# Graph-attention stack on one core: the projections at the ends of whole blocks, computed as seven products of quarters in place of eight

## The chip, the cores and the metric

The kernel runs on one core of a Trainium2 chip. The metric is the device time of one launch in microseconds, the median of several runs. TensorE (PE) multiplies matrices, VectorE (DVE) and ScalarE (ACT) do element-wise work, GpSimd (POOL) does a few small tasks here, and SyncE's queue (SP) issues nearly all DMAs.

## What is computed

A node matrix x (3327 x 256, f32) goes through four graph layers over one adjacency matrix. Each layer adds its result to x and normalises the rows. The last of the four holds three attention passes, so the kernel counts six layers: "0" (cosine attention), "1" (GAT), "2" (query/key attention), and "3a", "3b", "3c" (GAT). The part that matters is a GAT pass:

```python
def _gat_layer(h, adj, W, a):
    Wh = h @ W
    f1 = Wh @ a[:F_out]
    f2 = Wh @ a[F_out:]
    e = jax.nn.leaky_relu(f1 + f2.T, ALPHA)
    att = jnp.where(adj > 0, e, NEG_INF)
    att = jax.nn.softmax(att, axis=1)
    h_prime = att @ Wh
    return jax.nn.elu(h_prime)
```

The kernel uses att @ (h @ W) = (att @ h) @ W: it multiplies the unprojected h with the attention weights first, and projects the finished rows with the 256 x 256 matrix W afterwards. This projection is what the change is about.

## The kernel before

**Tiling.** The rows are padded to 3328 = 26 tiles of 128 (`NT`). Output rows are made in seven blocks (`NB`): b = 0 to 5 of 512 rows (4 tiles), b = 6 of 256 rows (2 tiles). A block runs over the 26 source tiles j in 26 steps. The main loop (`for s, (L, b, j)` over `steps`, L1276) is the same for all six layers.

**One step of a GAT layer.** ScalarE makes `re` (L657) and VectorE makes the weights `e` of tile j, 128 x 512 (L668). TensorE multiplies: four matmuls of 257 columns, one for each row tile of the block, into the PSUM tiles `po` (L1337); the 257th column sums the weights. Steps are prepared `LA` = 2 steps ahead and more where buffers allow: `e` has five buffers, `re` three. Layers "2" and most of "0" use products of quarters already (Strassen, in Winograd's form): there `products` (L751, matmuls at L779) does two source tiles at once with 14 matmuls of 128 or 129 columns.

**The end of a block.** When the 26th step is issued, `finish(L, b, pos)` (L871) is appended to `pending`, and `advance()` runs it up to its next `yield` once per step. So the end of block b is spread over the steps of block b + 1. For a GAT layer the pieces are: reciprocals of the sums (L959, L962) and scaled copies `p4` (L963); `turn` (L827): two ScalarE copies into `planes` (L834), a transposing DMA (L837), a few steps of waiting, two VectorE copies into `pT4` (L844); then, one row tile a step, `projected(k)` (L986), and after it `activated(k)` (L1020). `projected` for one tile is

```python
pm = bank("pproj")
for h in range(2):
    nc.tensor.matmul(pm[:, :D], pT[:, h, :], w[L.w][:, h, :], start=(h == 0), stop=(h == 1))
src = pm[:, :D]
```

with ELU read out of PSUM: ScalarE's relu and exp (L1007, L1008) and VectorE's maximum (L1011 in hidden layers, L1014 with the residual in "1" and "3c"). Hidden layers then compute the scores for the next layer (`scores`, L591) and a running sum (L862). Layers "1" and "3c" take row statistics (L883, L884) and normalise (L1050). Layer "1" also turns the normalised rows, projects them for layer "2" (`pv`, L1080, L1087) and stores sums for layer "2" (`combine`, L690, L713).

At j = 22 (L1373; at j = 25 in the last block of layer "1") what is left in `pending` is run to its end.

**Pools and order.** `ps_b` has three PSUM banks, shared by `pproj`, `pv`, `psr` and others. The tag `x4k` has two buffers of 4 KB a partition, shared by `planes`, `pT4`, `tsum` and others; `acc` has two. After a hand-ordered start the instructions of each engine are put in order by a scheduler at build time, which keeps dependencies and tile lifetimes; the order of the text is only its input. Each engine then runs its list strictly in order.

Of the kernel before, what the change touches and what calls it, by code (L numbers as in the profile page):

```python
# [8 lines left out]
F32 = mybir.dt.float32  # L9
# [5 lines left out]
ALU = mybir.AluOpType  # L15
# [4 lines left out]
P = 128  # L20
D = 256
H = 128
# [11 lines left out]
def gnn_stack(ctx: ExitStack, tc: tile.TileContext, a: dict, N: int, out: bass.AP):  # L34
# [8 lines left out]
    nc = tc.nc  # L43
    NT = (N + P - 1) // P
    NP = NT * P
    NB = (NP + CH - 1) // CH
# [14 lines left out]
    work = ctx.enter_context(tc.tile_pool(name="work", bufs=2))  # L61
# [4 lines left out]
    def bank(name):  # L66
        return ps_b.tile([P, CH], F32, tag="pb", name=name)
# [3 lines left out]
    start = tc.manual_schedule(  # L71
        engines={engines.PE, engines.Activation, engines.DVE, engines.Pool}
    )
# [30 lines left out]
    FT = [big.tile([P, 2, CH], F32, name=f"ft{g}") for g in range(NB)]  # L104
# [26 lines left out]
    w = {}  # L131
# [695 lines left out]
    def turn(x4, n, out, steps=3):  # L827

        half = "p k (n t) -> p t k n"
        pl = work.tile([P, 4, 2, D], U16, tag="x4k", name="planes", bufs=2)
        for t in range(2):
            nc.scalar.copy(pl[:, :n, t, :], x4[:, :n, :].bitcast(U16).rearrange(half, t=2)[:, t])  # L834
        yield
        tr = work.tile([P, 16, P], U16, tag="stage", name="turned", bufs=4)
        nc.sync.dma_start_transpose(  # L837
            out=tr[:, : 4 * n, :], in_=pl[:, :n].rearrange("p k t n -> p (k t n)")
        )
        for _ in range(steps):  # L840
            yield
        trv = tr[:, : 4 * n, :].rearrange("p (k t h) i -> p t k h i", t=2, h=2)
        for t in range(2):
            nc.vector.tensor_copy(out(t), trv[:, t])  # L844
        yield

    def turn_steps(L, b):

        if L.key == "1":
            return 5 if b == NB - 2 else 3  # L850
        return 7 if b == NB - 2 else 4

    class Sum:


# [15 lines left out]
    def finish(L, b, pos):  # L871
# [76 lines left out]
        else:  # L948
# [25 lines left out]
            if L.key != "2":  # L974
                pT4 = work.tile([P, 4, 2, P], F32, tag="x4k", name="pT4", bufs=2)
                yield from turn(
                    p4,
                    n,
                    lambda t: pT4[:, :n].bitcast(U16).rearrange(
                        "p k h (i t) -> p t k h i", t=2  # L980
                    )[:, t],
                    turn_steps(L, b),
                )
                pTs = {k: pT4[:, k] for k in range(n)}

            def projected(k):  # L986

                if L.key == "2":
                    src = p4[:, k, :]
                else:  # L990
                    pm = bank("pproj")
                    pT = pTs.pop(k)
                    for h in range(2):
                        nc.tensor.matmul(  # L994
                            pm[:, :D],
                            pT[:, h, :],
                            w[L.w][:, h, :],
                            start=(h == 0),
                            stop=(h == 1),
                        )  # L1000
                    src = pm[:, :D]
                e = work.tile([P, D], F32, tag="elu_e", name="elu_e", bufs=2)
                if L.key == "2":
                    nc.vector.tensor_scalar(e, src, 0.0, None, ALU.min)
                    nc.scalar.activation(e, e, AF.Exp)
                else:
                    nc.scalar.activation(e, src, AF.Relu, scale=-1.0)  # L1007
                    nc.scalar.activation(e, e, AF.Exp, scale=-1.0)  # L1008
                if L.hidden:
                    y = work.tile([P, D], F32, tag="y", name="z", bufs=6)  # L1010
                    nc.vector.tensor_scalar(y, src, 0.0, None, ALU.max)  # L1011
                else:
                    y = work.tile([P, D], F32, tag="y", name="y", bufs=6)
                    nc.vector.scalar_tensor_tensor(  # L1014
                        y, src, 0.0, xr[k], ALU.max, ALU.add
                    )
                es[k] = e
                ys.append(y)
# [10 lines left out]
            for p in range(n + 2):  # L1029
                if p >= 2:  # L1030
                    activated(p - 2)
                    if b == NB - 2:
                        yield
                if 1 <= p <= n:
                    projected(p - 1)
                if p > 0:
                    yield
        if not L.hidden:
            v = cols.tile([P, 4], F32, tag="var", name="var")
            nc.vector.tensor_scalar(v[:, :n], st[:, :n, 1], LN_EPS, None, ALU.add)  # L1040
            r = cols.tile([P, 4], F32, tag="rstd", name="rstd")
# [7 lines left out]
            for k, t in enumerate(ts_):  # L1049
# [8 lines left out]
                if L.key == "3c":  # L1058
                    q = LASTP if t == NT - 1 else P
# [8 lines left out]
            if L.key == "1":  # L1068
# [8 lines left out]
                for k, t in enumerate(ts_):  # L1077
                    pm = bank("pv")
                    for h in range(2):
# [4 lines left out]
                            start=(h == 0),  # L1084
                            stop=(h == 1),
# [122 lines left out]
    def advance():  # L1208
        while pending:
            try:  # L1210
                next(pending[0])
                return
            except StopIteration:
                pending.popleft()
# [61 lines left out]
    for s, (L, b, j) in enumerate(steps):  # L1276
        last = L.key == "3c"
        end = last and b == NB - 1
# [39 lines left out]
        if end:  # L1318

            k, h = divmod(2 * j, NT)  # L1320
            for i in (h, h + 1):
# [4 lines left out]
                    start=(i == 0),  # L1326
                    stop=(i == NT - 1),
# [7 lines left out]
        elif not strassen(L, b):  # L1335
            for k in range(len(pos)):
# [4 lines left out]
                    start=(j == 0),  # L1341
                    stop=(j == NT - 1),
# [27 lines left out]
        if nb == NB:  # L1370
            nl, nb = (None if last else layers[L.i + 1]), 0
        begin = 2 if last and b == NB - 2 else 14
        if j == (25 if L.key == "1" and b == NB - 1 else 22) and not end:  # L1373
            while pending:
                advance()
        if nl is not None and nl.key != "0":
# [4 lines left out]
        if j == NT - 1:  # L1381
            if b == 0 and not last:
                nl = layers[L.i + 1]
                L.sum = Sum()
                if nl.is_gat:
                    if nl.key == "1":
                        while "row_1" not in w:
                            next(setup)
                    nl.gat = Gat(nl.key)
                    L.gat_next = nl.gat  # L1390
            if end:
                pending.append(finish_last(pos[1], xm, 1))
            else:
                pending.append(finish(L, b, pos))
            advance()
# [65 lines left out]
```

## Time and profile before

| | |
|---|---|
| Median of 3 runs | 2366.33 us (2365.47 to 2366.51) |
| The profiled execution: its time | 2367.45 us |
| The profiled execution: its span, first to last instruction | 2365.6 us |
| Mean granted TensorE clock | 0.998 |
| PE busy | 2342.0 us (99%) |
| DVE busy | 1598.1 us (68%) |
| ACT busy | 1223.0 us (52%) |

The profile is that of one execution, in microseconds from its first instruction. A matmul of f32 data appears as two MATMUL records, and each has a LDWEIGHTS record beside it (PEld), which overlaps. So 5616 records of L1337 are 2808 matmuls. Matmuls overlap in the pipeline, so the mean duration of one record is longer than the distance from one to the next; what a stretch of matmuls costs is read from the starts in the chain or in the timeline. One GAT step, eight records of L1337, takes 1.73 us.

### The profile page before, as it was taken

To read this page: it belongs to the slowest core of one execution; us is meant where nothing else is said; L and a number is where in the kernel's file an instruction comes from. 1 tells how busy PE (TensorE), PEld (TensorE's weight loads), DVE (VectorE), ACT (ScalarE), POOL (GpSimd) and SP (SyncE) were. 2 spreads that over 40 slices of the span, in tenths; PEclk is the share of its full clock that TensorE was granted. 3 is DMA by queue.
4 is the path that set the end of the run, shared out by engine and by line. 5 is a ranking of instruction groups with operands and counts; after the bars stand their busy time and mean duration, and the time that the engine had idled before them with its cause. 6 is when DMAs were issued, how large, how long until landed. Compare 5 with 4: busy or idle time off the path is not lost.

```text
span 2365.6 us, 33125 instructions
## 1 busy us (share of the span) xinstructions
PE 2342.0 (99%) x11965; PEld 1913.4 (81%) x11965; DVE 1598.1 (68%) x4245; ACT 1223.0 (52%) x1959; POOL 38.7 (2%) x156
## 2 busy tenths in 40 slices
PE   9999999999999999999999999999999999999997
PEld 6778877888888777767767798888888888888886
DVE  7789999856767667566566685556656555655665
ACT  4667777755555422222222255555655555655554
POOL 0000001000000000000000000000000000000000
PEclk9999999999999999999999999999999999999999
DMA  8655565423332322212212221211211111132120
GB/s 274 196 184 184 167 196 193 151 71 83 83 78 57 103 54 87 79 53 88 74 50 73 83 84 52 72 52 26 76 47 43 43 59 52 43 98 69 61 65 24
DMA packets 147288, 214.66 MB, mean 91 GB/s; under 512 B 76093, under 2 KB 101172, under 8 KB 142516
## 3 DMA queue, kind: packets, MB, share of 16 engines
q1 hardware_dynamic: 146852, 212.28, 29.7%
q8 instruction: 94, 1.54, 0.3%
q14 instruction: 70, 0.57, 0.1%
q10 hardware_dynamic: 272, 0.26, 0.0%
HBM read 167.53 MB, written 28.19 MB: 83 GB/s over the span
## 4 chain that ended last, share of the span: by engine, by line
PE 94%; DVE 3%; ACT 1%; DMA 1%; issue 1%; POOL 0%; SPq 0%; DVEq 0%; ACTq 0%
PE po L1337 49%; PE po L779 19%; PE ps L563 12%; PE ps L492 6%; PE pproj L994 3%; PE pv L1080 1%; PE pgq L522 1%; ACT re L657 1%; PE po L1322 1%; PE pk L353 0%; PE pq L317 0%; DVE e L668 0%; DMA stage<-in_adj_a 0%; DVE v L668 0%; DVE e L506 0%
## 5 line engine op out<-in xcount | busy, mean ns | idle before, releaser
L1337 PE MATMUL po<-v,e 128*128 128x257 f32 x5616 | 1251.7, 381 | 1.4 <-ACT p L963 1.3
L1337 PEld LDWEIGHTS po<-v,e 128*128 128x128 f32 x5616 | 1062.2, 190 | 168.4 <-issue 9.3
L657 ACT ACTIVATE re<-u,nrh,th 128x512 f32<-128x512 f32 (+1 forms) x728 | 555.4, 780 | 472.2 <-DVE e L668 466.9
L668 DVE SCALAR_TENSOR_TENSOR e<-re,rh,mask 128x512 f32<-128x512 f32 (+1 forms) x702 | 501.0, 718 | 373.2 <-PE po L1337 343.2
L563 PE MATMUL ps<-gT,ft 128*128 128x512 f32 (+1 forms) x728 | 307.4, 563 | 0.0
L571 ACT ACTIVATE ex<-ps,off 128x512 f32<-128x512 f32 (+1 forms) x182 | 119.1, 655 | 356.7 <-PE ps L563 356.0
L779 PE MATMUL po<-tsums,ssum 128*128 128x128 f32 (+1 forms) x1794 | 249.3, 275 | 0.0
L477 DVE SCALAR_TENSOR_TENSOR e<-ex,mask 128x512 f32<-128x512 f32 (+1 forms) x182 | 118.4, 651 | 163.7 <-ACT ex L571 162.8
L779 PEld LDWEIGHTS po<-tsums,ssum 128*128 128x128 f32 x1794 | 224.5, 192 | 0.7 <-ACT y L919 0.3
L563 PEld LDWEIGHTS ps<-gT,ft 128*128 128x128 f32 x728 | 132.1, 190 | 114.5 <-issue 111.7
L779 PEld LDWEIGHTS po<-v,e 128*128 128x128 f32 x1196 | 169.3, 191 | 67.2 <-issue 52.9
L779 PE MATMUL po<-v,e 128*128 128x129 f32 x1196 | 182.3, 275 | 0.0
L505 ACT ACTIVATE ex<-ps,rq 128x512 f32<-128x512 f32 (+1 forms) x183 | 118.8, 651 | 119.2 <-PE ps L492 110.8
L492 PE MATMUL ps<-ft,ft 128*128 128x512 f32 (+1 forms) x312 | 142.5, 561 | 0.0
L506 DVE SCALAR_TENSOR_TENSOR e<-ex,mask 128x512 f32<-128x512 f32 (+1 forms) x183 | 116.5, 642 | 31.6 <-ACT ex L505 30.7
L449 DVE CUSTOM_DVE_ANT_0 acc<-acc,stage 128x1024 uint16<-128x1024 uint16 (+1 forms) x168 | 108.5, 646 | 15.4 <-DMA stage<-in_adj_a 11.8
L779 PE MATMUL po<-v,ssum 128*128 128x128 f32 x598 | 92.3, 275 | 0.0
L779 PE MATMUL po<-tsums,e 128*128 128x128 f32 x598 | 92.1, 275 | 0.0
L436 ACT ACTIVATE mask<-pos 128x1024 uint8<-128x1024 bf16 (+1 forms) x87 | 86.3, 992 | 2.1
L435 ACT ACTIVATE pos<-stage 128x1024 bf16<-128x1024 int32 (+1 forms) x87 | 85.6, 984 | 1.2 <-DVE e L506 1.2
L994 PE MATMUL pproj<-w_l_w,pT 128*128 128x256 f32 x304 | 78.2, 380 | 2.7 <-DVE pT L844 2.7
L779 PEld LDWEIGHTS po<-v,ssum 128*128 128x128 f32 x598 | 79.4, 192 | 0.1
(254 smaller groups left out, 1797.1 us busy)
## 6 DMA issues: line engine op xcount, KB each, us to landing
mask<-mask_d SPq DMA_DIRECT2D x30, 1664.0 KB
stage<-in_adj_a SPq DMA_DIRECT2D x78, 512.0 KB
tsums<-t_d SPq DMA_DIRECT2D x152, 256.5 KB
mask_d<-mask SPq DMA_DIRECT2D x6, 1664.0 KB
u<-s_d SPq DMA_DIRECT2D x24, 256.0 KB
xT<-in_xT SPq DMA_DIRECT2D x10, 512.0 KB
mask<-mask_d SPq DMA_DIRECT2D x5, 832.0 KB
t_d<-tsums SPq DMA_DIRECT2D x14, 256.5 KB
```

The costliest lines, as they stand in the source:

```text
L449: nc.vector.tensor_tensor(acc, acc, st[:, h * wd : (h + 1) * wd], ALU.add)
L477: nc.vector.scalar_tensor_tensor(e[:, :wd], t_[:, :wd], 0.0, mask(b, j), ALU.add, ALU.mult)
L492: nc.tensor.matmul(ps[:, :wd], FT[j // 4][:, 0, (j % 4) * P : (j % 4 + 1) * P], FT[b][:, 1, :wd], start=True, stop=True,)
L505: nc.scalar.activation(t_[:, c], ps[:, c], AF.Exp, scale=rq[:, j : j + 1])
L506: nc.vector.scalar_tensor_tensor(e[:, c], t_[:, c], 0.0, mask(b, j)[:, c], ALU.add, ALU.mult)
L563: nc.tensor.matmul(ps[:, :wd], FT[j // 4][:, h, (j % 4) * P : (j % 4 + 1) * P], g[:, h, :wd], start=(h == 0), stop=(h == 1),)
L571: nc.scalar.activation(t_[:, :wd], ps[:, :wd], AF.Exp, bias=off, scale=1.0 / D**0.5)
L657: nc.scalar.activation(t_[:, :wd], self.u[b][:, :wd], AF.Relu, bias=self.nrh[:, j : j + 1], scale=self.th[:, j : j + 1],)
L668: nc.vector.scalar_tensor_tensor(e[:, :wd], t_[:, :wd], self.rh[:, j : j + 1], mask(b, j), ALU.add, ALU.mult,)
L779: nc.tensor.matmul(o, x, y, start=(p == 0 and g not in banks[:i]), stop=(p == NT // 2 - 1 and g not in banks[i + 1 :]),)
L994: nc.tensor.matmul(pm[:, :D], pT[:, h, :], w[L.w][:, h, :], start=(h == 0), stop=(h == 1),)
L1337: nc.tensor.matmul(pos[k], es[:, k * P : (k + 1) * P], V[L.i % 2][j], start=(j == 0), stop=(j == NT - 1),)
```

## The change

The projection of a whole block, b = 0 to 4 of each of the four GAT layers (20 blocks), is done for its four row tiles together. The 512 x 256 matrix turned into `pT4` is split by row tile (even or odd) and by half of the inner dimension, W by halves of both dimensions. `projected4` makes four sums of turned quarters (VectorE), seven products of two matmuls each, 128 x 128 x 128 (TensorE, three PSUM banks), and puts them together in a new SBUF tile `c4`: one copy on ScalarE and seven sums on VectorE. Four more `yield`s spread this over four more steps. ELU then reads `c4` in SBUF and not PSUM. Four sums of quarters of W are made once a layer (`sum_weights`) into the unused right half of the last `FT` tile. The point at which `pending` is run to its end is j = 25 in all blocks of layer "1". Blocks 5 and 6 of each layer keep the projection of before.

```diff
+    wsum = [
+        FT[NB - 1][:, i // 2, D + (i % 2) * H : D + (i % 2 + 1) * H] for i in range(4)
+    ]
+
+    def sum_weights(wt):
+        b11, b12, b21, b22 = (wt[:, h, o * H : (o + 1) * H] for h in range(2) for o in range(2))
+        t1, t2, t3, t4 = wsum
+        nc.vector.tensor_tensor(t1, b12, b11, ALU.subtract)
+        nc.vector.tensor_tensor(t3, b22, b12, ALU.subtract)
+        nc.vector.tensor_tensor(t2, b22, t1, ALU.subtract)
+        nc.vector.tensor_tensor(t4, t2, b21, ALU.subtract)
+
+    def projected4(pT4, wt, c4):
+
+        add, sub = ALU.add, ALU.subtract
+        av = pT4.rearrange("p (a k) h q -> p a k h q", k=2)
+        a11, a12, a21, a22 = (av[:, :, k, h, :] for k in range(2) for h in range(2))
+        x = work.tile([P, 4, D], F32, tag="acc", name="psums", bufs=2)
+        s1, s2, s3, s4 = (x[:, i, :].rearrange("p (a q) -> p a q", a=2) for i in range(4))
+        nc.vector.tensor_tensor(s3, a11, a21, sub)
+        nc.vector.tensor_tensor(s1, a21, a22, add)
+        nc.vector.tensor_tensor(s2, s1, a11, sub)
+        nc.vector.tensor_tensor(s4, a12, s2, sub)
+        yield
+        b11, b12, b21, b22 = (wt[:, h, o * H : (o + 1) * H] for h in range(2) for o in range(2))
+        t1, t2, t3, t4 = wsum
+        cv = c4.rearrange("p (a k) (o f) -> p a k o f", k=2, o=2)
+        c11, c12, c21, c22 = (cv[:, :, k, o, :] for k in range(2) for o in range(2))
+
+        def two(*pairs):
+
+            pm = bank("pproj")
+            for i, (l, r) in enumerate(pairs):
+                for k in range(2):
+                    nc.tensor.matmul(
+                        pm[:, (2 * i + k) * P : (2 * i + k + 1) * P],
+                        l[:, k, :],
+                        r,
+                        start=True,
+                        stop=True,
+                    )
+            v = pm.rearrange("p (i a f) -> p i a f", i=2, a=2)
+            return v[:, 0], v[:, 1]
+
+        m1, m2 = two((a11, b11), (a12, b21))
+        m6, m7 = two((s2, t2), (s3, t3))
+        yield
+        nc.scalar.copy(c22, m1)
+        nc.vector.tensor_tensor(c11, c22, m2, add)
+        nc.vector.tensor_tensor(c22, c22, m6, add)
+        nc.vector.tensor_tensor(c21, c22, m7, add)
+        m5, m4 = two((s1, t1), (a22, t4))
+        yield
+        nc.vector.tensor_tensor(c12, c22, m5, add)
+        nc.vector.tensor_tensor(c22, c21, m5, add)
+        nc.vector.tensor_tensor(c21, c21, m4, sub)
+        m3, _ = two((s4, b22))
+        yield
+        nc.vector.tensor_tensor(c12, c12, m3, add)
...
                 pTs = {k: pT4[:, k] for k in range(n)}
+                if b < NB - 2:
+                    c4 = work.tile([P, 4, D], F32, tag="x4k", name="c4", bufs=2)
+                    yield from projected4(pT4, w[L.w], c4)
...
                 if L.key == "2":
                     src = p4[:, k, :]
+                elif b < NB - 2:
+                    src = c4[:, k, :]
                 else:
...
-        if j == (25 if L.key == "1" and b == NB - 1 else 22) and not end:
+        if L.is_gat and (b, j) == (0, 22):
+            sum_weights(w[L.w])
+        if j == (25 if L.key == "1" else 22) and not end:
             while pending:
                 advance()
```

## The prediction, made before the result was known

> **What bounds the kernel now.** I read the busy table first, then TensorE's waits by stage, then the chain of work in two stretches, then the groups of instructions that the change touches.
>
> ```profile
> PE 2342.0 (99%) x11965; PEld 1913.4 (81%) x11965; DVE 1598.1 (68%) x4245; ACT 1223.0 (52%) x1959; POOL 38.7 (2%) x156
> ```
>
> ```profile
> 1460.00:1508.85 48.85, 48.85 (x227) 42.47 (x226) 28.63 (x64) 27.64 (x42) 0.00 (x0) 1.00 0.18 52
> ...
> 581.00:633.20 52.20, 52.20 (x241) 45.51 (x241) 35.11 (x84) 29.00 (x43) 1.33 (x2) 1.00 0.33 84
> ```
>
> The two lines below the page's are the busy time of one block of layer 3a and of one of layer 1; the columns are length, then PE, PEld, DVE, ACT and POOL busy. TensorE has no gap there. So in the 20 blocks that change, TensorE's own work is the time, and DVE has 17 to 20 us free a block.
>
> ```profile
> PE pproj L994 <- DVE pT L844: 3.3, 4, 1.4
> PE po L1337 <- ACT p L963: 1.3, 2, 0.6
> ```
>
> These are TensorE's longest waits for projections in the whole run. By window the four of L994 lie at 788.05 us, between 1600 and 1850, between 1850 and 2100, and after 2100: one at the end of each GAT layer, in blocks 5 or 6, which keep the old path. Nothing is to be won from waits, then, only from matmul time. That is read in the chain (start, length, records):
>
> ```profile
> 812.66 3.45 PE pv L1080 x16
> 816.12 3.43 PE ps L563 x8
> 819.55 3.12 PE po L779 x28
> ...
> 2138.87 0.86 PE pproj L994 x4
> 2139.73 1.73 PE po L1337 x8
> ```
>
> `pv` is eight matmuls of 256 columns, the shape of today's projection of a block: 3.45 us. L779 is 14 matmuls of 128 or 129 columns, the number and width that the change uses: 3.12 us. L994's four records at 0.86 us agree with the first (4 x 0.86 = 3.44).
>
> ```profile
> L730 DVE TENSOR_TENSOR ssum<-e,ssum 128x256 f32<-128x256 f32 x143 | 60.1, 420 | 2.6
> ...
> L1008 ACT ACTIVATE elu_e<-elu_e 128x256 f32<-128x256 f32 x102 | 42.4, 416 | 3.0
> ...
> L1007 ACT ACTIVATE elu_e<-pproj 128x256 f32<-128x256 f32 x102 | 37.2, 364 | 15.4 <-PE pproj L994 15.4
> ...
> L711 DVE TENSOR_TENSOR tsum<-v,tsum 128x128 f32<-128x128 f32 x12 | 3.4, 285 | 0.0
> ...
> L819 DVE TENSOR_TENSOR p<-p,po 128x256 f32<-128x256 f32 x6 | 2.5, 421 | 0.0
> ```
>
> These price the added sums: 0.42 us for 128x256, whether an operand lies in PSUM (L819) or not (L730). L1007 and L1008 are ScalarE's price from PSUM and from SBUF.
>
> **What the skill says.** "TensorE: Matmul & The Clock Gate", section "Wait — 56ns, not 53.3ns?", gives N/2.4 GHz + 2.5 ns from one warm matmul pass to the next. If a record of f32 is two passes, 256 columns give 213.3 + 2.5 = 215.8 ns a record (estimate); the trace has 3.45/16 = 215.6. For 128 columns it gives 109.2, and the trace has 3.12/28 = 111.4: so the narrow shape loses a little more. The page's "Back-to-back issue gap" warns that narrow matmuls, with a weight load each, run slower than that formula; here the loss is 2 ns a record, and I use the trace. "VectorE: DVE Perf Modes", section on the TRN2 errata, prices an f32 sum at (N+151)/0.96 ns, 424 ns for N = 256 (estimate); the trace has 420. "PSUM — Partial Sum Buffer", section on bank collisions, says that two engines must not touch one bank at once; that fits DVE waiting for ScalarE at L1014 (35.7 us in all) and L1011 (16.8), where both read `pproj`. On the new path ELU reads SBUF and these waits go, but DVE isn't the bound.
>
> **The change, part by part.**
>
> *Projection matmuls.* Removed: 8 matmuls a block, 16 records, 3.45 us. Added: 14 matmuls, 28 records, 3.12 us. The eight records of 129 columns in L779 make that at most 0.01 too long. The gain is 0.33 us a block; 20 blocks give 6.6 us, all on the path, as TensorE has no gap there.
>
> *Pieces.* The scheduled order of the new kernel puts 16 records after one step, 8 after the next and 4 after the one after that. In between stand the usual eight records of L1337. The trace of before mixes shapes at such edges everywhere (8 records of L563, 28 of L779, period 6.56 = 3.44 + 3.12) without a loss, so edges cost 0; bounds -0.05 to +0.1 us a block.
>
> *Sums on VectorE.* 4 + 7 = 11 a block at 0.42 is 4.6 us; 20 blocks 92 us. With 4 x 4 weight sums at 0.285 (4.6 us) DVE goes to about 1695 us, 72%. Cover: in a 3a block DVE is busy 28.6 of 48.85, so 33.2 of 48.5 after. What counts is whether an `e` comes late. `e` has five buffers, so L668 starts when TensorE has finished the step five earlier, and DVE has 6.9 us (four steps) before TensorE needs that `e`. I followed a hidden block through the new order. After `e` number n, DVE does 3, 3, then 5 operations (2 us), then the eleven of `activated` and `scores` in one batch (about 3.5 us). A step leaves it 1.73 - 0.75 = 0.98 us free, so it falls behind by 3 to 4 us at worst, and is level again some four steps later. That stays inside 6.9. Cost 0; if the cover failed, the excess would go to TensorE block by block.
>
> *Waits of TensorE.* Where DVE's order has the `pT4` copies after `e` number n, the first products now stand after TensorE's step n - 2, today after n - 3: one step more room, and they need nothing else. The products with s2 and s3 need three sums behind one more `e`. At the one block I followed in layer 1, L844 ends at 579.5 us in the trace of before; add 0.75 for `e` and 3 x 0.35 for the sums (sums that follow each other start 0.34 apart in the timeline): 581.3. TensorE reaches that product at 579.95 + 1.73 + 0.9 = 582.6. Slack 1.3 us. m5 and m4 need no new sum, m3 needs s4, a step earlier. Queued behind a late sum would be all of TensorE. I take 0, bounds 0 to 0.3 us a block.
>
> *One copy on ScalarE, and SBUF sources.* One copy at 0.36 and four relus at 0.416 in place of 0.364: 0.57 us a block, 11 us in all. The first sum on DVE (L904) waits for that copy, which stands behind a `re` in ScalarE's order: 0.8 + 0.4 us in which DVE's queue, the next `e` among it, stands still. TensorE is at the eight products (1.78 us) then, so the next `e` may not start anyway. Cost 0.
>
> *Weight sums.* The scheduler puts those for layer 1 into block 0 of layer 0, at about 41.5 us by the order, behind the load of W issued at 36.07 us. The DMA engines run empty at about 41 us (they move 14 GB/s and then 0 in the two slices from 40.9 to 41.6), so the load has landed. The other three stand among the sums of block 4 of the layer before and wait for m7 or m5 there, which the sums beside them wait for too. Cost 0, at worst 1 us once.
>
> *What moves.* In layer 1 four more yields push the normalisation, the second turn, `pv` and `combine` back by about four steps: `pv` from steps 18, 19 to 22, 23. On SP's queue the mask fetch (1.66 MB) now stands ahead of the two `tsum` stores, and these ahead of the next turn. `planes` reuses the first store's buffer and `pT4` the second's: the stores must land first. By the order the stores are issued some 7 and 4 us before `planes` starts (estimate from steps of 1.73 us), and a store and its neighbours took up to 6.3 us to land (issue at 561.54, the fetch behind it let go at 567.86, with the mask beside it). Behind a late turn stand L844, so DVE, so `e`. I take 0; bounds 0 to 2 us for each of 4 blocks. Running `pending` out at j = 25 adds no work.
>
> *Sum.* The profiled execution took 2367.45 us with a span of 2365.6. 2367.45 - 6.6 = 2360.8. It lay 1.1 us above the median of the runs, so the median goes to 2366.33 - 6.6 = 2359.7.
>
> **Rivals.**
>
> *Part of the gain is eaten* (s2 and s3 late, edges of the pieces, turns late in layer 1): 0.1 to 0.3 us a block gives back 2 to 6 us: 2361.7 to 2365.7, say 2363.5. For it: slack of about 1 us against DMA landings that scatter by as much (L844's waits are 0.5 to 2.8 us). Against: no wait in these blocks today.
>
> *VectorE becomes the bound at block ends: slower.* The batches hold up `e` for longer than its five buffers cover. It decides from 0.33 us of TensorE wait a block: beyond that the gain is gone. If the batch in `projected4` and `activated` runs 1 us past the cover in each block, that is 20 - 6.6 = +13 us: 2380. For it: DVE work per block grows by 16% and comes in lumps. Against: my count leaves 3 us of cover, and DVE's 52 us of waits at L1011 and L1014 mostly go.
>
> *The products don't get cheaper*, that is, 28 narrow records cost what 16 wide ones do: 2366. Against: L779 shows 3.12 us in this kernel, with the same operand sizes.
>
> **How the numbers follow.** The measurement can tell about 0.2%, 4.7 us: faster is under 2361.6, slower over 2371.1. Full gain 0.72 (2358.6 to 2361.3), part eaten 0.14, no cheaper products 0.03, VectorE bound 0.11. A small part of the second case still counts as faster, a small part of the first doesn't. No reason allows more than 6.7 us, so the low end is that plus the scatter of the runs; the high end takes in most of the second case.
>
> **What would show it.** Right: 28 records for a block in 3.1 us, blocks of 3a in about 48.5 us and of layer 1 in 51.9, PE busy near 2335, DVE near 1695, and no wait at the new products. Wrong: TensorE waiting for `psums` or `e` in blocks 0 to 4, `e` waiting less for TensorE because DVE is late, `planes` or L844 waiting long in layer 1, or a wait at the weight sums near 41 us.

## The result, and the profile after

The changed kernel takes 2361.33 us (median of 15 runs, 2359.92 to 2363.78), the kernel before beside it 2366.41 us (2365.47 to 2368.90). The ratio is 0.9979, 95% interval 0.9971 to 0.9987: 5.1 us gained, between 3.1 and 6.9. The profiled execution went from 2367.45 to 2362.33 us, its span from 2365.6 to 2360.6.

The busy table of the changed kernel, and the busy time of the same block of 3a as before and of a stretch one block long in layer 1, which lies nearly a block ahead of the one shown before (columns: length, then PE, PEld, DVE, ACT, POOL):

```profile
PE 2336.8 (99%) x12205; PEld 1916.7 (81%) x12205; DVE 1661.3 (70%) x4481; ACT 1222.2 (52%) x1979; POOL 38.2 (2%) x156
```

```profile
1457.86:1506.39 48.53, 48.53 (x239) 42.56 (x238) 31.77 (x76) 27.54 (x43) 0.00 (x0) 1.00 0.18 52
536.22:588.09 51.87, 51.87 (x254) 45.59 (x253) 38.08 (x96) 29.03 (x44) 0.77 (x2) 1.00 0.36 95
```

Each block is 0.32 to 0.33 us shorter (48.85 to 48.53, 52.20 to 51.87), and TensorE still has no gap in it, with VectorE about 3 us busier. The chain at the end of that block of 3a shows the three pieces of the new projection, with eight records of L1405 (the former L1337) between them:

```profile
1499.80 1.78 PE pproj L890 x16
1501.58 1.74 PE po L1405 x8
1503.32 0.89 PE pproj L890 x8
1504.21 1.74 PE po L1405 x8
1505.94 0.44 PE pproj L890 x4
```

1.78 + 0.89 + 0.44 = 3.11 us. These are 28 records of 0.111 us in place of 3.45 us for 16, and the steps between them are no longer than before. TensorE's waits from 520 us to the end:

```profile
PE pproj L1062 <- DVE pT L844: 4.8, 4, 1.5
PE po L1405 <- ACT p L1026: 1.3, 2, 0.7
```

No line names the new products (L890). But L1062, the old projection that blocks 5 and 6 keep, waits 4.8 us in four places, where L994 waited 3.3. Twenty times 0.33 is 6.6 us; the waits took 1.5 of it, and 5.1 remains. The groups that the sums touch:

```profile
L1079 DVE TENSOR_SCALAR z<-c 128x256 f32<-128x256 f32 x40 | 9.0, 288 | 0.3
L877 DVE TENSOR_TENSOR psums<-psums,pT 128x256 f32<-128x256 f32 x20 | 8.5, 425 | 0.7
...
L904 DVE TENSOR_TENSOR c<-c,pproj 128x256 f32<-128x256 f32 x20 | 8.4, 421 | 19.7 <-ACT c L903 19.6
```

**Where the 1.5 us went.** I followed the issue of each transposing DMA in GAT layers through both traces, since it falls once a block. The lead over the kernel before grows by 0.33 us a block, as it should, and shrinks at two places: by 0.4 us at the end of 3a and by 0.95 us at the end of 3b. There TensorE, as it comes to block 5's projection (old path, in the short block 6), waits longer for the turned rows. The timeline of TensorE at the second place, in the kernel before and in the changed one (start, length, idle time before it and what ended that):

```profile
2006.75 4.93 PE L1337 MATMUL po<-v,e 128*128 128x257 f32 x22
2012.27 1.13 PE L994 MATMUL pproj<-w_l_w,pT 128*128 128x256 f32 x4 [0.59 <-DVE pT L844]
```

```profile
2002.71 4.50 PE L1405 MATMUL po<-v,e 128*128 128x257 f32 x20
2008.74 1.13 PE L1062 MATMUL pproj<-w_l_w,pT 128*128 128x256 f32 x4 [1.53 <-DVE pT L844]
```

The wait is 1.53 us and not 0.59, because this turn's data arrived later: from its issue to VectorE's copy 5.25 us passed, where the kernel before had 4.29. The turn of block 5 in 3a took 4.75 us, 4.34 before. The code between issue and copy is the same in both kernels.

### The profile page after: what moved, and what is told of

Same layout as the page of the kernel before. It is cut to its first block, busy times and chain, and to the rows that moved or that the text cites. A ratio compares the mean times of both kernels' runs of the same rounds, so it can differ in the third digit from the quotient of the medians.

```text
span 2360.6 us, 33869 instructions
## 1 busy us (share of the span) xinstructions
PE 2336.8 (99%) x12205; PEld 1916.7 (81%) x12205; DVE 1661.3 (70%) x4481; ACT 1222.2 (52%) x1979; POOL 38.2 (2%) x156
## 4 chain that ended last, share of the span: by engine, by line
PE 94%; DVE 3%; ACT 1%; DMA 1%; issue 1%; POOL 0%; POOLq 0%; SPq 0%; DVEq 0%
PE po L1405 48%; PE po L779 20%; PE ps L563 12%; PE ps L492 6%; PE pproj L890 3%; PE pv L1148 1%; PE pgq L522 1%; ACT re L657 1%; DMA turned<-planes 1%; PE po L1390 1%; PE pk L353 1%; PE pq L317 0%; DVE e L668 0%; PE pproj L1062 0%; DVE v L668 0%
## 5 line engine op out<-in xcount | busy, mean ns | idle before, releaser
L1405 PE MATMUL po<-v,e 128*128 128x257 f32 x5616 | 1248.6, 381 | 1.5 <-ACT p L1026 1.3
L1405 PEld LDWEIGHTS po<-v,e 128*128 128x128 f32 x5616 | 1057.7, 190 | 165.3 <-issue 9.3
L563 PEld LDWEIGHTS ps<-gT,ft 128*128 128x128 f32 x728 | 132.0, 190 | 114.5 <-issue 111.7
L506 DVE SCALAR_TENSOR_TENSOR e<-ex,mask 128x512 f32<-128x512 f32 (+1 forms) x183 | 116.9, 644 | 33.6 <-ACT ex L505 32.7
L779 PEld LDWEIGHTS po<-tsums,e 128*128 128x128 f32 x598 | 79.3, 192 | 0.0
```

The source lines that it names most:

```text
L506: nc.vector.scalar_tensor_tensor(e[:, c], t_[:, c], 0.0, mask(b, j)[:, c], ALU.add, ALU.mult)
L563: nc.tensor.matmul(ps[:, :wd], FT[j // 4][:, h, (j % 4) * P : (j % 4 + 1) * P], g[:, h, :wd], start=(h == 0), stop=(h == 1),)
L779: nc.tensor.matmul(o, x, y, start=(p == 0 and g not in banks[:i]), stop=(p == NT // 2 - 1 and g not in banks[i + 1 :]),)
L1405: nc.tensor.matmul(pos[k], es[:, k * P : (k + 1) * P], V[L.i % 2][j], start=(j == 0), stop=(j == NT - 1),)
```

## Experiments

Theory A: TensorE gains 0.33 us in each of 20 blocks in full, and DMA landings that scatter by themselves took 1.5 us of it. Its rivals: the sums on VectorE eat it (B); products are partly hidden behind other waits (C); the reorder in layer 1 costs something (D); the late turns are no chance, the change makes them late (E).

Each ratio below is to the kernel before on the same chip. Besides the times I use a length from the trace, from the issue of the first turn in layer 1 to the last instruction. What lies ahead of that turn is the same code in all of these kernels, but for the four sums of W for layer 1 (0.28 us each), and in their profiled executions it took 518.4 to 521.0 us. The two kernels without these sums lie inside that scatter (520.5 and 520.1). The length behind it is 1845.12 us for the kernel before and 1840.05 for the changed one, 5.07 less. It scatters little: three executions of the changed kernel have 1839.98 to 1840.05.

**The changed kernel once more.** No edit.

> The changed kernel once more, unaltered, for its profile. In its first profile 1.5 of the 6.6 us that the shorter projections should bring were missing, and all of it was lost at the ends of two layers, where the transposing DMA of the block before the last two landed 0.4 us (end of the first GAT projection layer 3a) and 0.95 us (end of 3b) later than before. Theory A (landings scatter by themselves): the late turns stand at other places this time, the gain inside the blocks is 0.33 us each as before, and the span again falls by 4 to 7 us. Theory E (the change puts these two transfers where they collide): the same two turns are late again by the same amounts. Time in either case 2360 to 2363 us, 3 to 7 us under the kernel before.

2361.28 us, ratio 0.9979 (0.9970 to 0.9987). The same turns were late by the same amounts: 4.71 us (4.75 in the first profile) in 3a, 5.24 (5.25) in 3b. The length was 1839.98 us. So these two late turns are no chance; they belong to this kernel.

**Seven products in layer 1 alone.**

```diff
-                if b < NB - 2:
+                if b < NB - 2 and L.key == "1":
```

(and the same condition where `src` is chosen and at `sum_weights`)

> The seven products in layer 1 alone (5 of the 20 blocks), the eight in the three GAT layers; the mask fetches and the first scores of the next layer stay moved as in the change. Theory A: 5 x 0.33 = 1.65 us under the kernel before, nothing back from the four reordered steps. Rival D (the reorder around layer 1's end and its later turns of ft, which landed 5.3 to 6.0 us after issue beside other transfers, cost something): 0 or slower than before. Rival B (the sums on VectorE eat the gain): under 1 us gained.

2365.05 us, ratio 0.9994 (0.9986 to 1.0002), 1.3 us under the kernel before: too small for the times. The length is 1843.50, 1.62 us less, against 1.65 expected. The turns of `ft` in layer 1, which landed 5.3 to 6.0 us after issue in the first three whole blocks of the changed kernel (4.3 before), did so here too (5.6, 5.9, 6.0), and TensorE waited for none of them (its waits for pT are the 3.3 us of before). As far as the length tells, the reorder in layer 1 is free.

**The sums doubled.**

```diff
         nc.vector.tensor_tensor(c12, c12, m3, add)
+        for _ in range(11):
+            y = work.tile([P, D], F32, tag="ejunk", name="extra", bufs=2)
+            nc.vector.tensor_tensor(y, x[:, 0, :], x[:, 1, :], add)
```

> The change with eleven more VectorE sums of 128x256 in each of the 20 blocks, behind the last sum of the block, into a scratch tile that nothing reads: the sums of the change are doubled. Theory A (VectorE has room beside TensorE, and what it falls behind it catches up within the block): VectorE's busy time grows by 80 to 95 us, the time stays within 1 us of the changed kernel's. Rival B (the sums already cost what is missing): 3 us or more slower than the changed kernel, with new PE waits for e or pT in the blocks.

2359.91 us, ratio 0.9973 (0.9962 to 0.9983). The busy table:

```profile
PE 2336.2 (99%) x12205; PEld 1916.4 (81%) x12205; DVE 1720.9 (73%) x4701; ACT 1219.4 (52%) x1979; POOL 38.4 (2%) x156
```

VectorE is 60 us busier, less than the 80 to 95 expected (busy time counts overlapping instructions once; the sum of the durations grew by 82.9). TensorE has no new wait for `e` or sums; its two largest waits from 520 us on:

```profile
PE pproj L1065 <- DVE pT L844: 3.9, 4, 2.0
PE po L1408 <- ACT p L1029: 1.3, 2, 0.6
```

So VectorE's room is real, and rival B falls. But the time was not the same: it was 1.4 us *lower* than the changed kernel's on the same chip (2361.28), beyond the 1 us expected; the length, 1839.08 us, is 0.9 to 1.0 lower. The turns of block 5 in 3a and 3b took 4.36 and 4.27 us here; they were not late, and up to the last turn 6.55 us of the 6.6 were there. (At the very end 0.5 went again: the last turn of block 5, in 3c, took 4.79.) Why more work on VectorE should make a DMA land sooner was the question from here on.

**One product less.** The product m3 is left out, and the last sum takes the sum of rows s4 in its place, so one quarter of each projection is not computed:

```diff
-        m3, _ = two((s4, b22))
         yield
-        nc.vector.tensor_tensor(c12, c12, m3, add)
+        nc.vector.tensor_tensor(c12, c12, s4, add)
```

> The change with its last product left out in each block: the two matmuls of m3 are gone, and the sum that took m3 takes the sum of rows s4 in its place, so the upper right quarters of the projections are not the reference's. It prices one product inside this kernel. Theory A: each of the 20 blocks is shorter by four records of 0.1114 us, 0.446 us, and the time falls by 8.9 us against the changed kernel, 13 to 16 us against the one before. Rival C (products are partly hidden, TensorE waits elsewhere for what VectorE and ScalarE owe it): less than 5 us.

2351.26 us, ratio 0.9934 (0.9922 to 0.9947), 10.0 us under the changed kernel where 8.9 were expected. The chain at the end of the same block:

```profile
1495.74 1.78 PE pproj L890 x16
1497.52 1.74 PE po L1404 x8
1499.26 0.89 PE pproj L890 x8
1500.15 3.04 PE po L1404 x14
```

The four records are gone, and blocks are shorter by 0.446 us each. By the lengths it is 10.1 us (1840.05 to 1829.95). The other 1.2 us are the turns again: 4.36 and 4.31 us in this kernel, neither late. A product on TensorE counts in full; rival C falls.

**What the late turns have in common.** In the list of DMA packets I looked at what else moved while a turn was under way. This is the DMA view of the changed kernel for the 5.2 us of the late turn in 3b, from 2002.09 us (queue, kind: packets, MB, share of 16 engines):

```profile
q1 hardware_dynamic: 2080, 0.52, 52.6%
q14 instruction: 1, 0.01, 0.4%
```

One packet of 8 KB carries instructions. In the changed kernel 47 of queue 14's 58 fetches fall where VectorE, ScalarE or SP passes a record near number 64 (55 to 72) of each 128 in its program, and this one is VectorE's (its record 4547, waits counted, which is 35 x 128 + 67). Queue 8's 96 packets of 16 KB match TensorE's program: 24,410 records, some 256 to a packet. In the 11 profiles with whole turns, 198 turns of four tiles in 3a to 3c fall into two heaps. With no such packet between 0.3 and 4.03 us after issue: 161 turns, all within 4.25 to 4.41 us. With one (24 times of queue 8, 13 of queue 14): 37 turns, median 5.06 us, 33 of them 4.60 to 5.89, four within 4.32 to 4.42. The limit of 4.03 was chosen to fit, but the gap between the heaps was not. A longer program on VectorE moves its fetches to other places in the block, which would explain both faster kernels. Up to the issue of the turn of block 5 in 3a, the changed kernel has 3898 records on VectorE, that with doubled sums 4020, and that with six products 3923 (as many sums as the changed kernel, but more records of waits). That can be tried without more work in the blocks.

VectorE stands at its own fetch when the late turn is due, so it might be VectorE that is late and not the DMA. The trace tells: the semaphore for which the copy waits is raised in 16 steps, and in all 198 turns the copy starts 0.02 us after the last step. In the late turn in 3b fifteen of the steps had come 4.35 us after issue, as in a turn on time, and the last came at 5.22; in 3a the fifteenth came at 4.47 and the last at 4.72. Where a turn is late and its fetch began 0.6 to 3.7 us after issue, all 16 steps are late.

**24 places further.** Tiny sums that nothing reads, once, in layer 1:

```diff
+    pads = [24]
...
         nc.vector.tensor_tensor(c12, c12, m3, add)
+        for _ in range(pads.pop(0) if pads else 0):
+            y = work.tile([P, 1], F32, tag="pad", name="pad", bufs=2)
+            nc.vector.tensor_tensor(y, x[:, 0, :1], x[:, 1, :1], add)
```

> The change with 24 sums of one column on VectorE, into a scratch tile, at the end of the first block of layer 1: they do nothing but move VectorE's later instructions 24 places down its program. In both profiles of the changed kernel VectorE fetches 8 KB of instructions at every 128th of its records (when it passes number 64 to 67 of each 128), and both late turns of block 5 have such a fetch 3.9 us after issue, while VectorE stands at number 64 to 67. Theory E (the late landing is the fetch of VectorE's own instructions, a matter of where in the program it falls): with 24 places the turns of block 5 stand at 82 to 91 of 128, no fetch falls in them, they land 4.3 us after issue in 3a and 3b, the end of 3a and 3b lose nothing, and the time falls by 1.3 us, to 2359.9 us. Theory A in its first form (landings scatter by themselves) or a cost of the sums: no change, 2361.3 us.

**128 places further**, one whole fetch: `pads = [26, 26, 26, 25, 25]`.

> The same with 128 such sums, 26 or 25 at the end of each whole block of layer 1: one whole fetch. Theory E: the fetches fall where they fell in the changed kernel, the turns of block 5 of 3a and 3b are late again, by 0.4 and 0.95 us, and the time is the changed kernel's, 2361.3 us. If merely having more small work on VectorE made the doubled sums faster, 128 would be faster than 24 or as fast: 2359.9 us or less.

TensorE's waits with 24 places and with 128:

```profile
PE po L1410 <- ACT p L1031: 1.6, 3, 0.7
PE pproj L1067 <- DVE pT L844: 0.6, 1, 0.6
```

```profile
PE pproj L1067 <- DVE pT L844: 1.5, 1, 1.5
PE po L1410 <- ACT p L1031: 1.3, 2, 0.7
```

(These are from 1700 to 2100 us, where 3b ends.) In the trace the theory held: with 24 places the turns took 4.35 and 4.29 us, with 128 they took 4.76 and 5.26, and the lengths are 1839.00 and 1840.05. The times did not show it: 2361.38 us (ratio 0.9975, 0.9965 to 0.9985) and 2361.59 us (0.9974, 0.9964 to 0.9984). A difference of 0.2 where 1.4 was expected: a miss, or lost in the scatter of the beginning. Three more kernels of this kind, run together, follow.

**The changed kernel a third time, 60 places (`pads = [20, 20, 20]`), and 24 again.**

> The changed kernel a third time, beside the two kernels with shifted programs below, because the times of the run with 24 places (2361.38 us) did not show the 1.0 us that its trace showed against the run with 128. Its trace is expected as in the first two: the turns of block 5 of 3a and 3b land 4.7 and 5.25 us after issue, TensorE waits 4.7 to 4.8 us for pT. Time 5.1 us under the kernel before.

> The change with 60 sums of one column, 20 at the end of each of the first three whole blocks of layer 1. Theory E: the turns of block 5 of 3a and 3b stand at 118 to 127 of 128 of VectorE's records, away from the fetch at 64 to 67; they land 4.3 us after issue, TensorE's wait for pT falls from 4.8 to 3.4 us, and the time is 1.0 to 1.4 us under the changed kernel's on the same chip. If the time is the changed kernel's although the trace shows the wait gone, the profiled execution's gain isn't in the others and stays open.

> The kernel with 24 places again, same chip as the changed kernel: 1.0 us under it if what the trace shows holds for every execution; no difference (under 0.4 us) if something gives it back.

2362.06, 2360.63 and 2360.37 us on one chip (ratios 0.9979, 0.9970 to 0.9987; 0.9973, 0.9962 to 0.9983; 0.9972, 0.9961 to 0.9983): 1.4 and 1.7 us under the changed kernel. The lengths are 1840.01, 1838.70 and 1839.04. The timeline of the kernel with 60 places at the end of 3b:

```profile
2002.74 3.85 PE L1410 MATMUL po<-v,e 128*128 128x257 f32 x17
2007.16 1.13 PE L1067 MATMUL pproj<-w_l_w,pT 128*128 128x256 f32 x4 [0.57 <-DVE pT L844]
```

and its DMA view while that turn was under way, with no instruction packet:

```profile
q1 hardware_dynamic: 2080, 0.52, 54.3%
```

The wait is 0.57 us, as in the kernel before. Over all runs, the kernels whose two turns are late lie 5.1, 5.1, 5.5 and 5.5 us under the kernel before of their chip, and those whose turns are not late 5.7, 6.5, 6.9 and 7.2. That agrees with the traces. The interval of each ratio is wider than the effect. Within each of the three groups that ran on one chip together, the mean of the executions without late turns lies 1.4, 0.05 and 1.45 us under the mean of those with them (standard errors 0.34, 0.41 and 0.38, from the scatter of the executions); weighted together that is 1.0 us with a standard error of 0.2. With 24 places 0.3 us were lost elsewhere, both times, early in 3b (the third wait of L1410 above, near 1804 us). Just ahead of it stands number 63 of 128 of VectorE's records, an `e` that started after 1.33 us of idle time and not the 0.98 of the changed kernel; whether a fetch is behind that was not tried.

**The turn of block 5 in two halves.**

```diff
+        for g in range(parts):
+            c = slice(g * m, (g + 1) * m)
+            for t in range(2):
+                nc.scalar.copy(
+                    pl[:, c, t, :], x4[:, c, :].bitcast(U16).rearrange(half, t=2)[:, t]
+                )
+            if parts == 1:
+                yield
+            nc.sync.dma_start_transpose(
+                out=tr[:, 4 * m * g : 4 * m * (g + 1), :],
+                in_=pl[:, c].rearrange("p k t n -> p (k t n)"),
+            )
...
```

(`parts` is 2 for b = 5 and 1 elsewhere, `m` = n // parts; VectorE copies by halves too. With halves there is no `yield` between ScalarE's copies and the issue.)

> The change with the turn of block 5 in every GAT layer cut into two: two pairs of copies on ScalarE, two transposing DMAs of two tiles, four copies of 128x512 on VectorE in place of two of 128x1024. A turn of two tiles lands 3.1 us after issue, one of four 4.3. Theory A/E: the first projection of block 5 needs only the first half, so TensorE's waits at it (0.7, 1.0, 1.5 and 1.5 us in the four layers, 4.7 in all) go, as far as nothing else in the chain from planes to the next layer's first scores is late: 2357 to 2361 us. If the halves queue behind each other and the next thing (VectorE's copies, the ELU steps) is as late: no change, 2361.3 us.

> Both: the split turn and the 24 places. Theory E: the fetch is away from the turns, so what the split doesn't hide of the 1.4 us is gained on top: 2356 to 2360 us, the fastest of the kernels so far. If the split takes all: the same as the split turn alone.

> The kernel before (eight products, no sums) with the split turn of block 5 alone. TensorE waited 3.3 us in four places for pT there. If the split's gain has nothing to do with the seven products: 3 us under the kernel before, 2363 to 2364 us, and the split and the seven products add up to the split changed kernel's 9.7 us. If the split only takes back what the products' kernel lost: no change, 2366.4 us.

2357.42 us (ratio 0.9956, 0.9944 to 0.9969) for the changed kernel with halves, 2357.17 us (0.9955, 0.9943 to 0.9968) with 24 places besides, and 2363.58 us (0.9984, 0.9977 to 0.9990) for the kernel before with halves. VectorE's timeline with halves in 3a, and TensorE's in 3b:

```profile
1683.47 0.79 DVE L855 COPY pT<-turned 128x512 uint16<-128x512 uint16 x2 [0.28 <-DMA turned<-planes]
...
1685.06 0.80 DVE L855 COPY pT<-turned 128x512 uint16<-128x512 uint16 x2 [0.43 <-DMA turned<-planes]
```

```profile
1997.73 6.23 PE L1417 MATMUL po<-v,e 128*128 128x257 f32 x28
2003.80 1.03 PE L1074 MATMUL pproj<-w_l_w,pT 128*128 128x256 f32 x4
```

In 3a the first half was issued at 1680.18 us and copied 3.3 us later, 1.6 us ahead of the second, and TensorE passes into the projection without a wait, here and in 3b. TensorE's waits in this kernel, from 520 us on:

```profile
PE po L1417 <- ACT p L1037: 1.5, 2, 0.8
PE pn L545 <- DVE g L542: 1.1, 1, 1.1
```

All four waits for pT are gone. In layer 1 that wins nothing, since a wait of 1.1 us at L545 stands behind it, but the ends of 3a, 3b and 3c win 0.75, 0.8 and 1.8 us over the kernel before. The kernel before with halves has the same wait in layer 1, and none for pT:

```profile
PE pn L545 <- DVE g L542: 1.1, 1, 1.1
```

It is not the first half alone that wins this. In 3a both halves are copied by 1685.86 us and the projection begins at 1686.68, in 3b the two moments are 2002.87 and 2003.80. The whole turn is done sooner, and the edit does two things for that. Turns of two tiles land sooner, and ScalarE makes `planes` sooner: at the end of 3a two `re` stand ahead of `planes` in the kernel before (1683.69 and 1684.56 us), and with halves they stand behind it. ScalarE in the kernel before, and in that kernel with halves (its next `re` starts at 1685.68):

```profile
1684.56 0.59 ACT L657 ACTIVATE re<-u,nrh,th 128x256 f32<-128x256 f32 x1
1685.05 1.98 ACT L834 COPY planes<-p 128x1024 uint16<-128x1024 uint16 x2
```

```profile
1683.26 0.62 ACT L838 COPY planes<-p 128x512 uint16<-128x512 uint16 x1
...
1684.13 1.66 ACT L838 COPY planes<-p 128x512 uint16<-128x512 uint16 x3
```

The second execution runs 0.28 us ahead here. With that taken off, the second half is issued 0.66 us ahead of the whole turn of before and copied 1.83 us ahead, where TensorE had waited 0.64. So the earlier issue alone might have removed this wait of the kernel before; no run has it without the halves.

By the lengths the halves save 4.8 us in the changed kernel (1840.05 to 1835.25) and 3.6 in the kernel before (1845.12 to 1841.48), and the times say 4.2 to 4.6 and 4.0. The 24 places add nothing in the sum (1835.22). Block by block they win 0.25 us at the end of 3a and 0.1 at the end of 3b, so the halves hide most of what the fetch delays and not all, and they lose as much in a wait of 0.3 us early in 3a, where `e` again stands at number 63 of 128. Split and products add up: 3.6 and the forecast 6.6 make 10.2, against 9.9 for both together. This is the fastest version that computes every product, 9.7 to 9.9 us under the kernel before.

## Why the prediction was right

*Projection matmuls, 0.33 us a block:* right, 3.45 to 3.11 us: block by block the lead grows by 0.32 to 0.34 us in 3a to 3c, and by 1.64 over the five of layer 1. *Pieces, 0:* right, the steps between them take 1.74 us. *The waits of TensorE for sums, 0:* right, no wait names L890. *Moves in layer 1, 0:* right in cost, with the layer-1 run. The later turns that I feared came (5.3 to 6.0 us), and TensorE did not wait for them. *Weight sums, 0:* right as far as the trace tells. Three of the four times one of them waited for a product, 2.3 us in all, and TensorE waited for none.

*Sums on VectorE, cost 0:* right, and the doubled sums show that as much again has room. But the size in the text was off: VectorE's busy time was to go to 1695 us and went to 1661.3. The durations of its instructions grew by 95.1 us in sum (1795.5 to 1890.6), as reckoned, but busy time counts overlap once, and these instructions overlap: two sums that don't need each other (L875 and L876) last 0.42 us and start 0.34 apart. Besides, `z` takes 288 ns from SBUF and took 424 from PSUM, which I hadn't counted. *ScalarE, +11 us:* off for the same reason. Its busy time went from 1223.0 to 1222.2, with 7.0 us of new copies in it; the sum of its durations grew by 9.2 (1301.6 to 1310.8). *The waits for ScalarE at L1014 and L1011 go:* 35.7 and 16.8 us became 6.6 and 5.3, and the new copy brought 19.6 us at L904, about what I gave for each block (18 waits, 1.1 us mean). What I had not seen: VectorE's `e` now waits for ScalarE's `re` 37 times, 32.7 us in all, where it did so 14 times, 10.9 us. It cost nothing, as no TensorE wait names `e`.

The prediction's estimate of 215.8 ns for a record takes two passes and adds the 2.5 ns of the formula it quotes once. With them twice it is 218.3 ns for 256 columns and 111.7 for 128; the traces have 215.6 and 111.1 to 111.4, so neither reading fits both widths. Nothing rested on it, as the price came from the trace.

*The sum, 6.6 us:* the time lay 1.6 us higher than forecast, inside the range, and 6.6 lies inside the interval of the gain (3.1 to 6.9). What the sum lacked is not in any of its terms: 1.4 us at two turns that the change doesn't touch, caught by VectorE's instruction fetches because the change made VectorE's program longer. How much was lost there was luck: with 60 records more on VectorE it is nothing, and nothing in the prediction bore on it. The measured 2361.33 us lies at the upper end of what the prediction gave to the full gain (2358.6 to 2361.3). The rival "part is eaten" named late turns, but in layer 1; it named the wrong turns and its 2 to 6 us was too much. "Nothing is to be won from waits" was wrong: I had taken the waits of L994 as a fixed 3.3 us. They are the end of a chain, from `planes` through the DMA to the first projection, without slack, and the split turn won 3.6 us there in the kernel before.

## What to carry to other kernels

Where TensorE has no gap, price a product by the starts of its records in the chain; here that gain held in every block. Whether VectorE has room is settled by doubling the added work. When a small gain is partly missing, compare landmarks of the two traces block by block: here that led straight to two DMAs. A DMA on a chain that TensorE waits for is worth making smaller and issuing sooner: by the times the two together won 4.0 to 4.6 us here, nearly as much as the change itself (5.1).

## What was not expected of the hardware

The traces show engines that fetch their instructions by DMA while they run (queue 8 in 16 KB, queue 14 in 8 KB). A transposing DMA of four tiles that meets such a fetch is late in 33 of 37 cases, by 0.3 to 1.6 us (161 turns without: 4.25 to 4.41 us, median 4.32; 37 with: median 5.06). For VectorE's fetches this is shown by moving them: 24 and 60 records ahead took them out of the two turns, 128 put them back. For the fetches of queue 8 it is only seen that the two go together; no run moved TensorE's program alone. In the three profiles of the changed kernel the two turns took 4.75, 4.71, 4.73 and 5.25, 5.24, 5.26 us. Other turns differ from one execution to the next: one in 3b took 4.27 and 4.89 us in the two executions of the kernel with 24 places, as queue 8's fetch fell 0.1 us before its issue or 0.7 after. So two kernels can differ by 1 us for the mere length of a program.

How one packet of 0.3 to 1.3 us delays the landing is open in part. In the late turn in 3b the packet started 3.87 us after issue, when all but two of the turn's own packets had started; these two started as it ended, at 4.17 and 4.18, and only the last of the 16 steps of the semaphore was late. Why that step came 1.0 us behind them, and why four of 37 turns weren't late, no run tried.
